# Last pair's early columns in two wide sets, both groups in one product, and a new order for the last norm, scans and scatters of the attention

## The chip, the cores and the metric

The kernel runs on one core of a Trainium2 chip. The metric is the device time of one execution in microseconds; the time before is the median of three runs. Lower is better.

## The reference, cut to what matters

An input `x` of 128 graphs with 64 nodes and 256 features goes through four layers, each with a residual and a layer norm. All arithmetic is in float32.

```python
x = layernorm(x + L0(x, adj))   # graph attention
x = layernorm(x + L1(x, adj))   # attention over 512 edges, 4 heads
x = layernorm(x + L2(x, adj))   # aggregation with A_hat, 256->512->256 with batch norms
x = layernorm(x + L3(x, adj))   # two graph convolutions, then windows of an LSTM

# L1: one score per edge and head, a softmax over the edges with one source, a weighted sum of values
e = einsum(leaky_relu(Xq[:, src] + Xq[:, dst]), a) + log(A0[src, dst] + eps)
attn = exp(e - max_by_src) / sum_by_src
Y = segment_sum(attn * Xv[:, dst], src) @ W_out.T

# L2, first step
agg = einsum('nm,bmd->bnd', A_hat, x)

# L3, after the convolutions gave h [128, 64, 256]
for p in (1, 2, 3, 4):                     # length of a window
    nw = 64 // p
    wins = h[:, :nw * p].reshape(128 * nw, p, 256)
    last = lstm_last(Wih[p-1], Whh[p-1], ..., wins)   # p steps, gates i, f, g, o
    h[:, w * p + p - 1] = last             # the last column of every window is replaced
```

For the change two places matter: the end of the edge attention (L1) with the aggregation of L2 after it, and the first step of the windows of lengths 2, 3 and 4 in the last LSTM pair. The windows of length `p` read the columns that the windows of length `p-1` have just replaced.

## The kernel before, in words

**Attention and the middle layers.** The 8192 rows are cut into 16 blocks `q` of 512 rows (`NQ`). A first long loop runs the attention of L0 and the edge scores of L1 block by block. Two blocks share one softmax `S` (`BPS = 2`), so there are eight of them. Its three parts are `l1_softmax` (lines 362 to 376: one product `L365`, an addition, two scans and a subtraction on VectorE, an exponential on ScalarE), `l1_sums` (two scans, `L380`, `L381`) and `l1_weights` (from line 383: eight transposes on TensorE, `L389`, a reciprocal `L395`, four multiplications `L397`, four indirect DMAs `L401` that scatter the weights into the table in DRAM, and two loads `ld` of that table, `L407`). For each block three further functions use the result: `v_a` (a copy of `ld` on GpSimd, `L414`, and 64 products `L422`), `v_b` (16 products with `wout`, `L436`, the residual, the layer norm with its statistics on VectorE and its powers and scaling on GpSimd, `L86` and `L100`, and a store) and `v_c` (64 small products `L456` with `aht`: the aggregation of L2).

In the loop these lag by three blocks (`LAG`). After it, what is left is the softmax of `S = 7` and `v_b(12)`, `v_c(12)` and `v_a`, `v_b`, `v_c` of blocks 13 to 15. They are traced one after another, each followed by an entry of `fill`: seven `up_block`s, products of L2's first matrix for a block whose aggregation is done (16 product instructions `L751` each), and then four larger jobs `up_job`. The last pool of the loop is closed after the softmax, and its five PSUM banks then serve the `pz` tiles of `fill`.

**Order.** `given` puts what a function traces behind the latest instruction of earlier `given` calls, on each engine by itself. An entry of `fill` isn't under `given`: the framework places its instructions where it expects an engine to be free, so parts of it can come ahead of a `given` function that was traced before it. On one engine the order is then fixed; an instruction that isn't ready holds up what is behind it.

**LSTM.** The 128 graphs are handled in eight groups of 16 (`GB`), two groups at a time: four pairs (`NP`). `H` holds a pair as `[128 features, 2 groups, 2 feature halves, 64 columns, 16 graphs]`. Windows of length 1 come first (`L1365`), then length 2 in two runs of 16 windows, length 3 with 21 windows, and length 4 with 16. The first step of a window has no hidden state: `plain` makes the three gates `g`, `i`, `o` by direct products (`begin`, `L1488`), with two halves `m` of a gate, two feature halves `k` of the input, and two groups `g`. Later steps use a seven-product scheme (`L1533`). In the trace each product of 32-bit numbers is two instructions.

A gate half of both groups fits into one PSUM bank of 512 columns when `2 * nw * GB <= 512`, that is for lengths 2 and 4. Then `joint` is true; both groups share one bank and one activation (`L1503`), but `begin` still issues one product for each group.

The last step of a window writes its result into `H` in four pieces (`L1438`): feature half 0 of group 0, half 1 of group 1, half 0 of group 1, half 1 of group 0. The next length's `plain` needs them. In the last pair there is no work of a next pair to put between, so `late_columns` splits the windows into columns that the running step doesn't write (`free`) and the others (`rest`). For gate `g` and half of gate `i` the free columns are issued ahead; the other gates go through all sets in one go. For length 3 the sets are windows 0 to 9, windows 10, 12, ... 20, and the late windows 11, 13, ... 19. For length 4 they are 0, 3, ... 15, then 1, 4, ... 13, and the late 2, 5, ... 14.

Of the kernel before, what the change touches and what calls it, by code (L numbers as in the profile page):

```python
# [21 lines left out]
KD = D // P  # L22
# [4 lines left out]
NQ = 16  # L27
# [14 lines left out]
def kernel(ctx: ExitStack, tc: tile.TileContext, i, out):  # L42
    nc = tc.nc
# [66 lines left out]
    def given(do, *args, **more):  # L110
        traced = nc.cur_bb.bb.instructions
        first = len(traced)
        with ExitStack() as order:
            for e in latest.values():
                order.enter_context(tc.issue_after(e))
            r = do(*args, **more)
        for t in traced[first:]:
            if t.engine in (mybir.EngineType.PE, mybir.EngineType.DVE, mybir.EngineType.Activation,
                            mybir.EngineType.Pool):
                latest[t.engine] = t  # L120
        return r
# [8 lines left out]
    with ExitStack() as two:  # L130
# [29 lines left out]
        class su:  # L160

            free = (NQ - NA) * 2 * QT
# [498 lines left out]
        LAG = BPS + 1  # L661
# [20 lines left out]
        for q in range(NQ):  # L682
            S = q // BPS - 1 if q % BPS == 0 else -1
# [16 lines left out]
        sums(q)  # L700
        S = NQ // BPS - 1
        given(l1_softmax, S)
        given(l1_sums, S)
        given(l1_weights, S)
        ph.close()


# [193 lines left out]
        def tile_sums(b):  # L901

            t2, t3, t4 = rooms[next(rooms_at) % len(rooms)]
            t1 = b(0, 1)
            given(nc.gpsimd.tensor_tensor, t3, b(1, 1), t1, OP.subtract)
            given(nc.vector.tensor_sub, t1, t1, b(0, 0))
            given(nc.gpsimd.tensor_tensor, t2, b(1, 1), t1, OP.subtract)
            given(nc.gpsimd.tensor_tensor, t4, b(1, 0), t2, OP.subtract)
            return [t1, t2, t3, t4]
# [12 lines left out]
        def inputs(q):  # L922
            return lambda k, n: Aq(q + n)[:, k * QT:(k + 1) * QT]
# [10 lines left out]
        def one(q):  # L934
            return lambda: up_block(q)

        def pair(q, g):
            return lambda: up_job(q, g, T[q])

        fill = [one(n) for n in range(7)] + [pair(n, g) for n in (7, 9) for g in range(2)]  # L940
        sums_at = {5: 7, 7: 9}
        for n, (do, q) in enumerate([(v_b, NQ - LAG - 1), (v_c, NQ - LAG - 1)] + [
                (do, q) for q in range(NQ - LAG, NQ) for do in (v_a, v_b, v_c)]):
            given(do, q, *[False] * (do == v_c))
            fill[n]()
            if n in sums_at:
                T[sums_at[n]] = tile_sums(inputs(sums_at[n]))
        q = NQ - LAST - 1
# [212 lines left out]
    def lbank(shape):  # L1161
        return ps.tile([P] + shape, F32, name="l", bufs=6)
# [180 lines left out]
    def gate_of(n):  # L1343
        return "ifgo".index(n), AF.Tanh if n == "g" else AF.Sigmoid

    def lstm(pair):
# [36 lines left out]
        for p in range(2, SKIP + 1):  # L1383
            w = weights_of[pair, p]
            runs = [(r, N // p // 2) for r in (0, N // p // 2)] if p == 2 else [(0, N // p)]
            nw = runs[0][1]
# [6 lines left out]
            def inp(r, s, m):  # L1393

                w0 = runs[r][0] * p
                return H[:, :, m, w0:w0 + nw * p, :].rearrange("p n (w s) b -> p n w s b", s=p)[:, :, :, s, :]
# [65 lines left out]
            begun = {}  # L1462

            def late_columns(r):

                if pair < NP - 1 or p == 2 or r:
                    return [slice(0, nw)], []
                mine, q = range(nw), p - 1
                wrote = [w for w in mine if w * p % q == q - 1 and w * p < N // q * q and (q > 2 or w * p >= N // 2)]
                step = wrote[1] - wrote[0]  # L1470
                assert wrote == list(range(wrote[0], nw, step))[:len(wrote)]
                head = wrote[0] // step * step
                free = [slice(0, head)] * (head > 0) + [slice(head + n, nw, step) for n in range(step)
                                                        if head + n != wrote[0]]
                return free, [slice(wrote[0], nw, step)]

            def begin(n, r, ms, parts):

                at, _ = gate_of(n)
                joint = 2 * nw * GB <= QT  # L1480
                for m in ms:
                    if (n, m) not in begun:
                        begun[n, m] = lbank([2, nw, GB]) if joint else [lbank([nw, GB]) for g in range(2)]
                    for g in range(2):
                        for c in parts:
                            for k in range(KD):
                                b = begun[n, m][:, g] if joint else begun[n, m][g]
                                nc.tensor.matmul(b[:, c], w.raw[0][:, k, at, m, :],  # L1488
                                                 inp(r, 0, k)[:, g, c], start=k == 0, stop=k == KD - 1)

            def plain(n, r, tiles):

                t = tiles[n] = rows()
                free, rest = late_columns(r)
                for m in (1, 0):
                    f, b = bias_of(n, m)
                    begin(n, r, (m,), rest if (n, m) in begun else free + rest)
                    banks = begun.pop((n, m))
                    if isinstance(banks, list):
                        for g in range(2):  # L1500
                            nc.scalar.activation(t[m][:, g], banks[g], f, bias=b)
                    else:
                        nc.scalar.activation(t[m], banks, f, bias=b)  # L1503
                for m in (1, 0):
                    finish(n, r, 0, tiles, m)
                    tanh(n, tiles, m)
# [69 lines left out]
            for r in range(len(runs)):  # L1576
                if p > 2:
                    yield "gap", unit
                for s in range(p):
                    last = s == p - 1  # L1580
                    if s == 0:
                        tiles = {}
                        free, rest = late_columns(r)
                        if rest:
                            given(begin, "g", r, (1, 0), free)
                            given(begin, "i", r, (1,), free)
# [139 lines left out]
    for k in range(NP):  # L1726
# [5 lines left out]
        for n in range(2):  # L1732
            g = k * 2 + n
# [61 lines left out]
```

## Time and profile before

| | us |
|---|---|
| median of three runs (lowest, highest) | 2063.9 (2063.64, 2063.99) |
| the profiled execution, whole | 2062.37 |
| its span, first to last instruction | 2060.1 |
| TensorE busy in it | 1966.5 (95%) |
| VectorE, ScalarE, GpSimd busy | 1186.3, 968.4, 807.0 |
| mean granted TensorE clock | 0.983 |

The page of the profile gives busy times and the chain of waits that ended last, followed back from the last instruction. TensorE holds 75% of that chain and VectorE 14%. Queries of the trace then show single stretches: the chain in order of time, one engine's instructions in order of time, and groups of instructions by line with their tile shapes kept apart. Times in them are microseconds from the start of the span. In the group rows the durations of matmuls overlap, since a matmul's record starts before the one ahead of it has left the array; the spacing of a run of matmuls is read from the chain, which counts no time twice.

### The profile page before, as it was taken

Reading aid. Unit: us, or ns where it says so; the run is one execution under the profiler, and the core shown is the slowest. Engines: PE = TensorE matmul, PEld = TensorE weight load, DVE = VectorE, ACT = ScalarE, POOL = GpSimd, SP = SyncE. Lnnn points to the kernel's source line nnn. Section 1 sums busy time; section 2 is a strip of 40 time slices with the busy share of each in tenths; the row PEclk is TensorE's granted clock in tenths of the full one; section 3 lists DMA queues with packets and bytes.
Section 4 is the critical chain, followed back from the end, with each engine's and each line's share of the span. In section 5 each row is a group of like instructions: output and inputs, shape, how many; then the busy total and the mean of one; then the engine's idle time right before and its main releaser. Section 6 shows DMA issues by size and latency. Waiting matters only on the chain.

```text
span 2060.1 us, 31841 instructions
## 1 busy us (share of the span) xinstructions
PE 1966.5 (95%) x11775; PEld 1387.8 (67%) x11775; DVE 1186.3 (58%) x2683; ACT 968.4 (47%) x1852; POOL 807.0 (39%) x961
## 2 busy tenths in 40 slices
PE   5999999998899999999999999999999999999996
PEld 4667677675454445687688587678587678588785
DVE  7466666554457555564566664566674466443556
ACT  3766766665245633543333644333644343533333
POOL 1123343343245534363445253245243345133254
PEclk9999999999899998999999999999999999999998
DMA  6354343332202027251232622032521032301022
GB/s 159 56 71 72 71 74 54 55 55 44 34 22 60 34 97 264 92 179 52 93 133 69 205 90 87 11 138 63 194 78 77 1 128 63 128 1 77 1 66 67
DMA packets 235962, 170.71 MB, mean 83 GB/s; under 512 B 150560, under 2 KB 213536, under 8 KB 232480
## 3 DMA queue, kind: packets, MB, share of 16 engines
q1 hardware_dynamic: 233952, 166.72, 28.8%
q8 instruction: 93, 1.52, 0.3%
q0 software_dynamic: 1024, 1.05, 0.2%
q10 hardware_dynamic: 832, 0.92, 0.1%
q14 instruction: 61, 0.50, 0.1%
HBM read 107.82 MB, written 60.82 MB: 82 GB/s over the span
## 4 chain that ended last, share of the span: by engine, by line
PE 75%; DVE 14%; POOL 4%; ACT 3%; issue 3%; DMA 1%; SPq 0%; DVEq 0%; POOLq 0%; ACTq 0%
PE l L1533 27%; PE l L1488 9%; PE l L1365 8%; PE pz L822 4%; PE e L346 3%; PE m L318 3%; PE pz L751 2%; PE g L1328 2%; PE m L321 2%; PE pz L1014 2%; PE z L355 2%; DVE ln_st L95 1%; PE g L1316 1%; PE m L253 1%; PE g L1246 1%
## 5 line engine op out<-in xcount | busy, mean ns | idle before, releaser
L1533 PE MATMUL l<-xs,wx 128*128 128x256 f32 (+1 forms) x896 | 276.7, 399 | 5.8 <-DVE gate L1552 4.8
L1533 PE MATMUL l<-hs,wh 128*128 128x256 f32 (+1 forms) x896 | 275.3, 399 | 2.7 <-DVE hs L1402 2.6
L86 POOL TENSOR_TENSOR ln_rs<-ln_rs,mhalf 128x2 f32<-128x2 f32 (+2 forms) x98 | 83.7, 854 | 456.1 <-DVE ln_rs L98 447.0
L1548 ACT ACTIVATE kept<-l 128x256 f32<-128x256 f32 (+1 forms) x224 | 88.7, 403 | 339.7 <-PE l L1533 338.5
L1533 PE MATMUL l<-H,wx 128*128 128x256 f32 (+1 forms) x672 | 210.3, 401 | 3.4 <-DVE gate L1561 3.4
L1533 PE MATMUL l<-hid,wh 128*128 128x256 f32 (+1 forms) x672 | 208.7, 399 | 0.0
L1533 PEld LDWEIGHTS l<-xs,wx 128*128 128x128 f32 x896 | 168.8, 190 | 50.1 <-POOL st L100 6.6
L1533 PEld LDWEIGHTS l<-hs,wh 128*128 128x128 f32 x896 | 169.3, 190 | 45.4 <-DVE hs L1402 5.2
L1488 PE MATMUL l<-H,wx 128*128 128x256 f32 (+4 forms) x960 | 193.6, 360 | 0.9 <-DVE H L1438 0.9
L1566 ACT ACTIVATE gate<-gate,bias 128x512 f32<-128x512 f32 (+1 forms) x280 | 170.5, 657 | 37.4 <-DVE gate L1557 31.1
L1488 PEld LDWEIGHTS l<-H,wx 128*128 128x128 f32 x960 | 160.3, 190 | 33.5 <-issue 4.1
L1365 PE MATMUL l<-H,wih 128*128 128x512 f32 x384 | 167.2, 596 | 0.0
L357 ACT ACTIVATE u<-z 128x1024 f32<-128x1024 f32 x128 | 130.4, 1025 | 63.4 <-PE z L355 62.4
L1533 PEld LDWEIGHTS l<-H,wx 128*128 128x128 f32 x672 | 125.8, 190 | 38.2 <-DVE gate L1561 7.4
L1533 PEld LDWEIGHTS l<-hid,wh 128*128 128x128 f32 x672 | 127.2, 190 | 32.0 <-issue 2.6
L1365 PEld LDWEIGHTS l<-H,wih 128*128 128x128 f32 x384 | 73.2, 191 | 89.9 <-issue 82.9
L1556 POOL TENSOR_TENSOR gate<-gate,kept 128x256 f32<-128x256 f32 (+1 forms) x84 | 65.0, 774 | 158.8 <-DVE kept L1554 158.7
L329 DVE TENSOR_TENSOR qs<-m,qs 64x256 fp32r<-64x256 f32 x128 | 54.0, 422 | 108.6 <-ACT qs L328 106.4
L1406 POOL TENSOR_TENSOR hs<-hid 128x256 f32<-128x256 f32 (+1 forms) x28 | 25.9, 926 | 200.4 <-DVE hid L1435 116.7
L355 PE MATMUL z<-gath_r,qs 128*128 128x512 f32 x256 | 100.8, 481 | 0.5 <-issue 0.4
L1460 ACT ACTIVATE gate<-cell 128x512 f32<-128x512 f32 (+1 forms) x88 | 58.6, 666 | 84.2 <-DVE cell L1452 60.5
L1550 DVE TENSOR_TENSOR gate<-l,kept 128x256 f32<-128x256 f32 (+1 forms) x112 | 49.1, 438 | 72.2 <-ACT gate L1566 44.1
(336 smaller groups left out, 3821.2 us busy)
## 6 DMA issues: line engine op xcount, KB each, us to landing
wx<-sums SPq DMA_DIRECT2D x9, 2048.0 KB
wh<-sums SPq DMA_DIRECT2D x9, 1792.0 KB
way<-st SPq DMA_DIRECT2D x54, 256.0 KB
st<-way SPq DMA_DIRECT2D x216, 64.0 KB
xin<-in_x SPq DMA_DIRECT2D x16, 512.0 KB
ld<-table SPq DMA_DIRECT2D x16, 512.0 KB
x_dram<-y SPq DMA_DIRECT2D x16, 512.0 KB
x2r<-x_dram SPq DMA_DIRECT2D x32, 256.0 KB
```

The costliest lines, as they stand in the source:

```text
L86: nc.gpsimd.tensor_tensor(dst, dst, mhalf[:, :n], OP.pow)
L318: nc.tensor.matmul(pq, xT[:, k, c * P:(c + 1) * P], wq[:, k, :], start=k == 0, stop=k == KD - 1)
L346: nc.tensor.matmul(pes[S][n * CG:(n + 1) * CG, :], apad[:, k, CG - HEADS - r0:2 * CG - HEADS - r0], u[:, k, :], start=r0 == 0 and k == 0, ...
L355: nc.tensor.matmul(z[:, k, :], L1[q]["qs"][c][:, s, k * P:(k + 1) * P], gath_r, start=True, stop=True)
L357: nc.scalar.activation(u, z, AF.Relu)
L822: nc.tensor.matmul(self.bank[at], lhs, rhs, start=first and n == 0, stop=n == len(self.terms) - 1, skip_group_check=True)
L1365: nc.tensor.matmul(b, wih1[:, k, mw * P:(mw + 1) * P], Hw[:, k], start=k == 0, stop=k == KD - 1)
L1488: nc.tensor.matmul(b[:, c], w.raw[0][:, k, at, m, :], inp(r, 0, k)[:, g, c], start=k == 0, stop=k == KD - 1)
L1533: nc.tensor.matmul(self.banks[j], lhs, rhs, start=src == 0, stop=src == 1)
L1548: nc.scalar.activation(self.keep(j), b, AF.Copy)
L1556: e.tensor_tensor(t[0][:, 1], t[0][:, 1], k[5], OP.add)
L1566: given(lambda: nc.scalar.activation(dst, dst, f, bias=b))
```

## The change

Three edits.

1. `l1_sums` and `l1_weights` of the last softmax leave their place at the end of the loop. The new order is `l1_softmax(7)`, `v_b(12)`, `up_block(0)`, `l1_sums(7)`, `up_block(1)`, `v_c(12)`, `l1_weights(7)`, and then blocks 13 to 15 as before, each function followed by the same entry of `fill` as before.
2. `late_columns` makes two contiguous sets instead of strided ones when the first late window isn't among the first few. For length 3 they are windows 0 to 10 (free) and 11 to 20 (rest). For length 4 the sets stay as they are.
3. In `begin`, when a bank is joint, one product covers both groups. This applies to lengths 2 and 4 in all four pairs.

```diff
         sums(q)
         S = NQ // BPS - 1
         given(l1_softmax, S)
-        given(l1_sums, S)
-        given(l1_weights, S)
         ph.close()
...
         fill = [one(n) for n in range(7)] + [pair(n, g) for n in (7, 9) for g in range(2)]
-        sums_at = {5: 7, 7: 9}
-        for n, (do, q) in enumerate([(v_b, NQ - LAG - 1), (v_c, NQ - LAG - 1)] + [
-                (do, q) for q in range(NQ - LAG, NQ) for do in (v_a, v_b, v_c)]):
+        given(v_b, NQ - LAG - 1)
+        fill.pop(0)()
+        given(l1_sums, S)
+        fill.pop(0)()
+        given(v_c, NQ - LAG - 1, False)
+        given(l1_weights, S)
+        sums_at = {3: 7, 5: 9}
+        for n, (do, q) in enumerate([(do, q) for q in range(NQ - LAG, NQ) for do in (v_a, v_b, v_c)]):
             given(do, q, *[False] * (do == v_c))
             fill[n]()
             if n in sums_at:
...
                 wrote = [w for w in mine if w * p % q == q - 1 and w * p < N // q * q and (q > 2 or w * p >= N // 2)]
                 step = wrote[1] - wrote[0]
                 assert wrote == list(range(wrote[0], nw, step))[:len(wrote)]
-                head = wrote[0] // step * step
-                free = [slice(0, head)] * (head > 0) + [slice(head + n, nw, step) for n in range(step)
-                                                        if head + n != wrote[0]]
-                return free, [slice(wrote[0], nw, step)]
+                if wrote[0] < step:
+                    return [slice(n, nw, step) for n in range(step) if n != wrote[0]], [slice(wrote[0], nw, step)]
+                return [slice(0, wrote[0])], [slice(wrote[0], nw)]
...
-                    for g in range(2):
+                    for g in range(1 if joint else 2):
                         for c in parts:
                             for k in range(KD):
-                                b = begun[n, m][:, g] if joint else begun[n, m][g]
-                                nc.tensor.matmul(b[:, c], w.raw[0][:, k, at, m, :],
-                                                 inp(r, 0, k)[:, g, c], start=k == 0, stop=k == KD - 1)
+                                x = inp(r, 0, k)
+                                b, x = (begun[n, m][:, :, c], x[:, :, c]) if joint else (begun[n, m][g][:, c], x[:, g, c])
+                                nc.tensor.matmul(b, w.raw[0][:, k, at, m, :], x, start=k == 0, stop=k == KD - 1)
```

## The prediction

> **What bounds the kernel now.** I read the page first: the busy line and the chain of waits that ended last.
>
> ```profile
> PE 1966.5 (95%) x11775; PEld 1387.8 (67%) x11775; DVE 1186.3 (58%) x2683; ACT 968.4 (47%) x1852; POOL 807.0 (39%) x961
> PE 75%; DVE 14%; POOL 4%; ACT 3%; issue 3%; DMA 1%; SPq 0%; DVEq 0%; POOLq 0%; ACTq 0%
> ```
>
> TensorE is the bound nearly everywhere, so an edit pays where it shortens TensorE's own stream or removes one of its gaps. The chain in order of time shows the stages that edits 2 and 3 touch (start, length, what).
>
> ```profile
> 1796.80 10.36 PE l L1488 x48
> 1831.34 10.36 PE l L1488 x48
> 1865.87 17.20 PE l L1488 x144
> 1883.07 26.05 PE l L1533 x92
> 1947.82 16.04 PE l L1488 x144
> 1963.86 13.01 PE l L1533 x60
> ```
>
> The first two are a first step of length 2 (256 columns an instruction), the third is length 3 of the last pair, the fifth length 4 of the last pair. All are unbroken TensorE with TensorE on both sides. 10.36 / 48 is 216 ns for 256 columns, 0.843 ns a column. A third of the columns of length 4 would take far less than 16.04 / 144 = 111 ns. The group rows with shapes kept apart say how narrow they are.
>
> ```profile
> L1488 PE MATMUL l<-H,wx 128*128 128x80 f32 x144 | 18.9, 273 | 0.0
> L1488 PE MATMUL l<-H,wx 128*128 128x96 f32 x96 | 14.4, 273 | 0.0
> L1488 PE MATMUL l<-H,wx 128*128 128x160 f32 x48 | 8.9, 307 | 0.0
> ```
>
> 80 and 96 columns should stream in 67 and 81 ns but are 111 ns apart: a floor per instruction. With 160 columns at 135 ns, length 3 should take 48 x 135 + 96 x 111 = 17.1 us; the chain has 17.20.
>
> For edit 1 I read TensorE in order of time, then GpSimd (start, duration, instruction; idle before it and what ended that).
>
> ```profile
> 527.69 1.07 PE L389 MATMUL m<-ident,e 128*128 128x128 f32 x4 [2.01 <-ACT e L375]
> 535.47 6.17 PE L751 MATMUL pz<-A,w 128*128 128x512 f32 x14
> 545.74 2.31 PE L456 MATMUL m<-aht,y 64*64 64x64 f32 x64 [4.10 <-POOL y L100]
> 547.98 4.65 PE L751 MATMUL pz<-A,w 128*128 128x512 f32 x6
> ...
> 533.72 1.08 POOL L401 DMA_INDIRECT table<-at,place  x1 [8.56 <-DVE at L397]
> 537.24 0.96 POOL L401 DMA_INDIRECT table<-at,place  x1 [2.43 <-DVE ln_mv L96]
> 540.12 0.96 POOL L401 DMA_INDIRECT table<-at,place  x1 [1.93 <-DMA table<-at,place]
> 542.99 0.96 POOL L401 DMA_INDIRECT table<-at,place  x1 [1.91 <-DMA table<-at,place]
> 543.98 1.05 POOL L86 TENSOR_TENSOR ln_rs<-ln_rs,mhalf 128x4 f32<-128x4 f32 x1
> 547.25 1.93 POOL L414 COPY am<-ld 128x1024 f32<-128x1024 f32 x1
> ```
>
> TensorE waits 2.01 us for the softmax and 4.10 us for the norm of block 12, which stands on GpSimd behind four scatters that take from 533.72 to 543.95.
>
> **What the Trainium skill says.** *TensorE: Matmul & The Clock Gate*, section "LDWEIGHTS (loading the stationary operand)": a weight load costs its columns / 1.2 in ns, so 107 ns for 128; the 111 ns floor agrees. The same page, "Part 1: The HAM clock gate": an idle window of about 3.4 us halves TensorE's clock until it has been busy as long again. The trace agrees: after the 4.10 us gap the 64 products take 2.31 us, against 1.09 at 571.11. *PSUM — Partial Sum Buffer*, "The four PSUM rules": one product writes at most one bank, 512 float32 columns. The joint product of lengths 2 and 4 is 2 x 16 x 16 = 512 and fits. *DMA: Bandwidth & Descriptors*, "Anatomy of one DMA — SWDGE (gpsimd) path": about 2.0 us fixed for each; the scatters land 2.13 us after issue and each waits for the one before, 2.9 us apart.
>
> **Edit 2, length 3 of the last pair.** 144 instructions become 96: 48 of 176 columns and 48 of 160, both over the floor. 48 x 0.148 + 48 x 0.135 = 13.6 us, against 17.20: 3.6 us gone. The early part shrinks from 24 x 135 + 24 x 111 = 5.9 us to 24 x 0.148 = 3.56 us, and it covers the four writes of `H`. These run in VectorE's list as one row, 1867.93 with 1.42 us, so to 1869.35; the early part would end at 1869.43. No wait is left (bound 0 to 0.3).
>
> **Edit 3, length 4 of the last pair.** 144 instructions become 72: 24 of 192 columns (162 ns) and 48 of 160 (135 ns), 10.4 us against 16.04: 5.7 us gone. The early part becomes 12 x 162 + 12 x 135 = 3.56 us, to 1951.38, and the last write of `H` ends at 1951.76 (1950.00 with 1.76). One pair of products needs only the earlier writes; 0.2 us stays (bound 0 to 0.5). Both stages are followed by TensorE's own work. ScalarE has 6.4 us and VectorE 6.4 us of work in those 16, so neither becomes the bound. The DMA round trip of an output group that VectorE waits for after 1977 begins behind instructions that TensorE feeds and moves with them. Sum for the last pair: 3.6 + 5.7 - 0.2 = 9.1 us on the path.
>
> **Edit 3 elsewhere.** From 256 to 512 columns nothing is won: 96 products of 512 columns of length 1 take 41.20 us, 429 ns each, twice 216. Fewer weight loads cost nothing as they lie beside the stream. But a joint product waits for both groups. At the start of length 4 in pairs 0 to 2, TensorE issues four instructions at 1031.86, before the last write of `H`, and goes on at 1033.18. The first joint product needs the third write of four, which ends near 1032.7; from there 10.36 us run through, to 1043.1, where 1033.18 + 44 x 0.216 gave 1042.7. So +0.4 us, three times: 1.2 us (bound 0 to 1.8). At length 2 the columns read first were written earlier, and the second run's too: nothing.
>
> **Edit 1.** From 522.28 to 552.64, where `v_a(13)` starts, TensorE's work at full clock is 16 x 0.216 + 32 x 0.429 + 8 x 0.214 + 1.09 = 20.0 us; 10.4 us are lost, 6.1 in the two gaps and 4.3 to the halved clock. Afterwards: `v_b(12)`'s products are ready at once and go first (to 525.7), then two `up_block`s of 6.87 us (to 539.5). VectorE does the softmax, to 527.0, then the norm (4.3 us) among block statistics, then the two scans. GpSimd has nothing ahead of the norm, which is done by about 537; so `v_c(12)` and the transposes follow without a gap, to 542.2. Then the reciprocal and products (2 us), four scatters (544.3 to about 554.5) and, behind them on GpSimd, the copy `L414` for `v_a(13)` (1.93): ready at about 556. That is the new wait: what stood behind the scatters was the norm, now it is this copy. SP gains nothing and loses nothing: block 12's store comes earlier, the two loads of `ld` later, and `v_a(14)` that reads them came 26.7 us after `v_a(13)`.
>
> Between 542.2 and 556 TensorE can do `up_block(2)` and `(3)`, 13.7 us, if they are placed ahead of `v_a(13)`. Before, the framework put ten instructions of `up_block(1)` ahead of `v_c(12)`, 10.3 us of work behind the transposes where 14.4 were needed: it expected the scatters about 4 us too early. With the same error `v_a(13)` comes 4 us too early: a gap of 4 us and 2 to 3 us of halved clock, 6.9 in all instead of 10.4. I take 3.5 us gained. Bounds: -2.5 us if only `up_block(2)` comes ahead (gap near 9), +10 if no gap is left.
>
> **Sum.** The span goes from 2060.1 by -9.1 + 1.2 - 3.5 = -11.4 to 2048.7; with the 2.3 us around it (2062.37 - 2060.1) 2051.0. The median of the runs is 1.5 us over the profiled execution, so 2052.5.
>
> **Rivals.**
> - *The copy for `v_a(13)` takes the place of the norm in full.* For it: one queue on GpSimd, and the scatters start 10 us later than before. Against: two more blocks can cover it. Edit 1 then costs 2.5: 2063.9 - 9.1 + 1.2 + 2.5 = 2058.5.
> - *The scatters vanish behind the blocks.* Against: the misplaced `v_c(12)` above. 2063.9 - 9.1 + 1.2 - 10 = 2046.0.
> - *Length 4 gives its gain back* to the output's DMA round trip that VectorE waits for up to 1984.89. Against: its transfer starts from VectorE instructions that move along. 2052.5 + 5.5 = 2058.0.
> - *Slower: the joint product is held by writes it doesn't read.* Its operand spans both groups, with the columns just being written in between. If it waited for those, run 2 of length 2 would start after the four `H` writes, 1835.06 where TensorE is ready at 1831.34 (3.7 us), and run 1 about 1 us late; four pairs make 18.8 us, 2071.3. It decides from 11.4 us, 2.9 a pair. Against: at 1865.87 the strided set of windows 10, 12, ... is read between columns that are written until 1869.35, and TensorE doesn't stop.
>
> **How the numbers follow.** The forecast has 0.55 (own range 2049 to 2056), the rivals in their order 0.18, 0.12, 0.08, 0.07. With all bounds against it the gain is 8.5 - 1.8 - 2.5 = 4.2, 2059.7; with all for it 9.3 + 10 = 19.3, 2044.6. I take 2046 to 2060. A measurement here can't tell less than about 0.2%, 4.1 us, from no change. The first and third rival stand close to that line, so faster 0.83, the same 0.11, slower 0.06.
>
> **What would show it.** In the changed trace: 96 and 72 instructions in the last pair's two first steps, taking 13.6 to 13.9 and 10.4 to 10.9 us; no gap ahead of `v_c(12)`; a gap of about 4 us ahead of `v_a(13)`'s products, ended by GpSimd's copy; the first joint product of length 4 at about 1032.7 in the old count. Wrong would be a gap at a start of length 2, or last steps that end less than 8 us sooner, measured from the start of length 3 of the last pair.

## The result and the profile after

The changed kernel takes 2052.35 us (median of four runs, 2049.48 to 2053.71); the kernel before took 2063.94 beside it (four runs, 2063.64 to 2065.31). The ratio is 0.9941, with a 95% interval of 0.9923 to 0.9958. The profiled execution has a span of 2050.9 us against 2060.1, at the same mean TensorE clock, 0.983.

The page of the changed kernel, busy times and then the shares of the chain that ended last:

```profile
PE 1959.1 (96%) x11391; PEld 1329.2 (65%) x11391; DVE 1185.8 (58%) x2683; ACT 968.4 (47%) x1852; POOL 809.7 (39%) x961
PE 74%; DVE 13%; POOL 4%; ACT 4%; issue 3%; DMA 2%; SPq 1%; POOLq 0%; ACTq 0%; DVEq 0%
```

TensorE issues 384 instructions fewer, the other engines the same number. Its busy time falls by only 7.4 us. For 264 of those that went, two products of 256 columns became one of 512, which takes as long as the two.

The chain in order of time, at the stages shown before (start, length, what):

```profile
1797.74 10.30 PE l L1491 x24
1832.21 10.30 PE l L1491 x24
1866.69 13.68 PE l L1491 x96
1880.37 26.00 PE l L1535 x92
1945.07 10.83 PE l L1491 x72
1955.90 12.96 PE l L1535 x60
```

Length 2 has half the instructions and the same time, 10.30 us against 10.36, and nothing waits at its two starts. Length 3 of the last pair goes from 17.20 to 13.68 us and length 4 from 16.04 to 10.83. From the start of the one to the end of the other it is 89.21 us, against 97.99.

At length 4 of the first pair the chain runs through the writes of `H`, as it did before, and leaves them after the third instead of the fourth:

```profile
1030.76 0.42 DVE H L1441
1031.18 0.60 DVE hT L1321
1031.78 0.84 DVE H L1441 x2
1032.62 0.04 issue
1032.67 7.13 PE l L1491 x16
```

The first joint product starts at 1032.67, 0.05 us after the third write of `H` ended.

The end of the edge attention, TensorE and then GpSimd in order of time (start, duration, instruction; in brackets the idle time before it and what ended that):

```profile
543.08 1.16 PE L456 MATMUL m<-aht,y 64*64 64x64 f32 x64
544.17 0.66 PE L389 MATMUL m<-ident,e 128*128 128x128 f32 x4
...
545.96 12.18 PE L749 MATMUL pz<-A,w 128*128 128x512 f32 x28
560.65 1.16 PE L422 MATMUL m<-am,v 64*64 64x64 f32 x64 [2.50 <-POOL am L414]
...
573.10 2.08 PE L456 MATMUL m<-aht,y 64*64 64x64 f32 x64 [0.80 <-POOL y L100]
```

```profile
533.96 1.03 POOL L86 TENSOR_TENSOR ln_rs<-ln_rs,mhalf 128x4 f32<-128x4 f32 x1 [5.07 <-DVE ln_rs L98]
535.10 3.45 POOL L100 TENSOR_SCALAR y<-y,ln_rs 128x256 f32<-128x256 f32 x4
548.94 1.09 POOL L401 DMA_INDIRECT table<-at,place  x1 [10.39 <-DVE at L397]
...
557.70 0.96 POOL L401 DMA_INDIRECT table<-at,place  x1 [1.92 <-DVE st L755]
558.67 1.93 POOL L414 COPY am<-ld 128x1024 f32<-128x1024 f32 x1
...
572.50 2.17 POOL L100 TENSOR_SCALAR y<-y,ln_rs 128x256 f32<-128x256 f32 x4
```

Both old gaps are gone: `v_c(12)` and the transposes follow their predecessors. The norm of block 12 is done at 538.55, ten microseconds ahead of the first scatter. The queue of GpSimd now holds up the copy of `v_a(13)`, and TensorE waits 2.50 us for it. A second, shorter wait of 0.80 us stands ahead of `v_c(13)`; the 64 products after it take 2.08 us instead of 1.16.

In some spells the record grants TensorE only half of its clock (0.50); its products then take about twice as long (from 561.74 four of 512 columns take 3.45 us; at full clock, from 578.98, sixteen take 7.13). Two stretches of the changed kernel (window, its length, busy time and in brackets the instructions of TensorE, of its weight loads, VectorE, ScalarE and GpSimd; then the granted clock, DMA share, GB/s):

```profile
562.20:565.40 3.20, 3.20 (x5) 1.35 (x4) 0.69 (x1) 1.49 (x3) 0.00 (x0) 0.50 1.28 152
573.10:575.20 2.10, 1.86 (x65) 1.38 (x65) 0.00 (x0) 0.00 (x0) 2.10 (x4) 1.00 0.02 4
```

After the wait of 2.50 us the clock is at half. At `v_c(13)` it is full: its products take 2.08 us because they come in four groups, each when GpSimd has finished one of the four pieces of `y` (`L100`, 0.54 us apart).

Put together, the span moved by -9.2 us as follows. The changed stages gave -3.5 (length 3), -5.2 (length 4), +1.2 (joint products in pairs 0 to 2) and -5.0 (end of the attention), together -12.5. Code that both kernels share took 3.3 back: the last score products ended 3.7 us later (524.91 against 521.19), the code from L2's output to the last pair lost 1.0, and the rest of the last pair gained 1.4. The experiments show that 1.5 to 1.8 of the 5.0 us is such a difference too, and not the edit's.

### The profile page after: what moved, and what is told of

It reads as the page before. It is cut to its first block, busy times and chain, and to the rows that moved or that the text cites. A ratio compares the mean times of both kernels' runs of the same rounds, so it can differ in the third digit from the quotient of the medians.

```text
span 2050.9 us, 31078 instructions
## 1 busy us (share of the span) xinstructions
PE 1959.1 (96%) x11391; PEld 1329.2 (65%) x11391; DVE 1185.8 (58%) x2683; ACT 968.4 (47%) x1852; POOL 809.7 (39%) x961
## 4 chain that ended last, share of the span: by engine, by line
PE 74%; DVE 13%; POOL 4%; ACT 4%; issue 3%; DMA 2%; SPq 1%; POOLq 0%; ACTq 0%; DVEq 0%
PE l L1535 27%; PE l L1491 9%; PE l L1368 8%; PE pz L820 4%; PE e L346 3%; PE pz L749 3%; PE m L318 3%; PE g L1331 2%; PE pz L1017 2%; PE m L321 2%; PE z L355 2%; PE m L253 2%; PE m L436 1%; PE g L1319 1%; DVE ln_st L95 1%
## 5 line engine op out<-in xcount | busy, mean ns | idle before, releaser
L1568 ACT ACTIVATE gate<-gate,bias 128x512 f32<-128x512 f32 (+1 forms) x280 | 170.6, 657 | 37.4 <-DVE gate L1559 31.1
L1491 PE MATMUL l<-H,wx 128*128 128x512 f32 (+4 forms) x576 | 183.7, 475 | 2.2 <-DVE H L1441 2.2
L1535 PEld LDWEIGHTS l<-H,wx 128*128 128x128 f32 x672 | 125.9, 190 | 42.8 <-issue 7.4
L1491 PEld LDWEIGHTS l<-H,wx 128*128 128x128 f32 x576 | 100.9, 190 | 76.2 <-issue 53.6
```

Source lines behind the costliest of these rows:

```text
L1491: nc.tensor.matmul(b, w.raw[0][:, k, at, m, :], x, start=k == 0, stop=k == KD - 1)
L1535: nc.tensor.matmul(self.banks[j], lhs, rhs, start=src == 0, stop=src == 1)
L1568: given(lambda: nc.scalar.activation(dst, dst, f, bias=b))
```

## The experiments

In what follows, "the stretch" is measured in the trace, from the end of the last 16 score products to the first of the 60 products of L2's output (`L1014` before, `L1017` after). Before it is 144.58 us and after 139.59. Where an expectation counts from the start of those score products (143 for after, 148.1 for before), it is 1.9 to 3.6 us more, as their own clock differs; the readings here leave that out. Gains in us that stand beside a ratio are worked out from the ratio.

**Each edit alone.** Each of the three kernels is the kernel before with one edit of the diff: only edit 1, only `late_columns`, only `begin`.

> Edit 1 alone; the last pair as before. My theory: the stretch from the last score products (the final row of 16 e products, 517.66 before) to the first of the 60 products of line 1014 takes 143 us instead of 148.1, with a gap of 2 to 4 us ahead of the products of v_a(13); the last pair's first steps stay at 17.2 and 16.0 us; ratio to before about 0.9980. Rival (the gain of edit 1 is only a run-to-run difference): the stretch stays within 1 us of 148.1, ratio 1.0000.

Measured: 2056.74 us (20 runs) against 2061.26 for the kernel before (31 runs), a ratio of 0.9977 (0.9971 to 0.9984): 4.7 us, with bounds of 3.3 and 6.0. The stretch is 139.61 us, 5.0 less. That is far from a stretch that stays within 1 us, so the rival is out. Its wait is the one of the changed kernel:

```profile
557.89 1.16 PE L422 MATMUL m<-am,v 64*64 64x64 f32 x64 [2.52 <-POOL am L414]
```

> Edit 2 alone. My theory: the first step of length 3 in the last pair takes 13.6 to 13.8 us instead of 17.20, from 96 instructions instead of 144; length 4 stays at 16.0; all that follows comes 3.5 us earlier; ratio about 0.9983. Rival (VectorE's chain at the end of length 3 gives it back): the stage shrinks but the start of length 4 comes less than 2 us earlier.

Measured: 2055.55 us (10 runs), 0.9976 (0.9966 to 0.9985), which is 4.9 us (3.1 to 7.0). The chain shows length 3 shortened and length 4 as it was:

```profile
1864.59 13.68 PE l L1487 x96
...
1942.98 16.04 PE l L1487 x144
```

From the start of the one to the start of the other it is 78.39 us, against 81.95 before, so VectorE gives nothing back and the rival is out.

> Edit 3 alone. My theory: length 4 of the last pair 10.4 to 10.9 us instead of 16.04; in pairs 0 to 2 the time from the 80 products before the start of length 4 to the seven-product run after it grows from 44.24 to 44.6 us; net about 4.1 us gained, ratio 0.9980. Rival (a joint product is free everywhere): the stretch in pairs 0 to 2 stays at 44.2 us and the net gain is 5.2 us.

Measured: 2054.08 us (6 runs), 0.9966 (0.9953 to 0.9978), which is 7.0 us (4.5 to 9.7). Here length 3 is as it was and length 4 is short:

```profile
1864.35 17.20 PE l L1489 x144
...
1946.29 10.83 PE l L1489 x72
```

In pairs 0 to 2 the time from the 80 products to the seven-product run is 44.61, 44.62 and 44.48 us, against 44.24 before: the joint product isn't free there.

Edits 2 and 3 do in their stages what they do together, 3.5 and 5.2 us (4.1 with the three waits of 0.4). The timed gains are larger than that, and the three add up to 16.6 us where the whole change gives 11.6. The trace shows where the surplus lies: from the end of the score products to the first step of length 2 the code of the second and third kernel is that of before, yet this part takes 337.70 and 337.90 us in them and 341.06 before. Two of the places (before, then edit 3 alone):

```profile
777.34 5.17 PE L1316 MATMUL g<-hT,wg 128*128 128x512 f32 x8
...
808.84 6.51 PE L1365 MATMUL l<-H,wih 128*128 128x512 f32 x12
```

```profile
777.51 4.18 PE L1316 MATMUL g<-hT,wg 128*128 128x512 f32 x8
...
807.82 5.42 PE L1365 MATMUL l<-H,wih 128*128 128x512 f32 x12
```

The products are the same; the half-clock spells last longer in the first kernel. The stretches show it, in the columns explained above (before, then edit 3 alone):

```profile
770.00:820.00 50.00, 46.46 (x496) 28.90 (x497) 31.19 (x76) 19.65 (x33) 25.74 (x32) 0.86 0.69 248
```

```profile
770.00:820.00 50.00, 45.54 (x501) 27.83 (x502) 32.16 (x77) 20.09 (x33) 25.94 (x32) 0.95 0.71 253
```

The stretch at the end of the attention isn't free of this either: with its code unchanged it takes 142.82 us with edit 2 alone and 143.04 with edit 3 alone, where the kernel before has 144.58. With edit 1 alone the part from the score products to length 2 takes 337.30 us, and with all three 337.35. So in this part edits 2 and 3 gain over 3 us without touching its code, and edit 1 on top of them only some 0.5.

**The joint product only where the columns are split**, so not in pairs 0 to 2:

```diff
+                wide = joint and bool(late_columns(r)[1])
...
-                    for g in range(1 if joint else 2):
+                    for g in range(1 if wide else 2):
```

> The changed kernel, but with one product for both groups only where the windows are split into sets (length 4 of the last pair); elsewhere one product per group, as before. My theory: the stretch in pairs 0 to 2 goes back from 44.6 to 44.24 us, length 4 of the last pair stays at 10.8; 1.1 us faster than the changed kernel, ratio to before about 0.9936. Rival (the wait of the joint product lies beside other work): the same time as the changed kernel, and the sums of the stage differ by less than 0.2 us in each pair.

Measured: 2048.64 us (four runs), 0.9941 (0.9924 to 0.9957). From the start of the 80 products ahead of it to the first seven-product run, length 4 takes 44.24 us in pairs 0 to 2 of the kernel before, 44.62 to 44.64 after, and 44.24 here. Length 4 of the last pair keeps its 10.82 us. So the joint product costs 0.37 to 0.40 us in each of those pairs, 1.16 in all, and this kernel has them back; the timed runs can't tell it from the changed kernel (0.9941 both). The kernels below build on this one, except where stated.

**The scatters further back**, behind `v_a(13)`, and then behind `v_b(13)` as well:

```diff
         given(v_c, NQ - LAG - 1, False)
+        given(v_a, NQ - LAG)
+        fill.pop(0)()
         given(l1_weights, S)
```

The second kernel has `given(v_b, NQ - LAG)` and one more `fill.pop(0)()` after these two lines.

> The kernel with joint products only where the windows are split, and the weights of the last softmax (transposes, scatters, loads) moved one function further back, behind v_a(13). My theory: the copy for v_a(13) no longer stands behind the scatters, so its 2.5 us gap goes; the norm of block 13 now does, and as the framework expects the scatters about 4 us too early a gap of 1 to 4 us comes ahead of v_c(13). The stretch from the end of the last score products to the 60 products of line 1014 takes 138 to 140 us (139.5 in the changed kernel). Rival (the gap comes from the scatters' own transfer holding the table, not from GpSimd's order): the gap ahead of v_a(13) stays.

Measured: 2051.58 us against 2064.74, 0.9940 (0.9923 to 0.9956): no better than 0.9941. The wait of `v_a(13)` is gone, which rules the rival out, and a longer one stands ahead of `v_c(13)`, whose norm is now behind the scatters:

```profile
565.68 2.32 PE L456 MATMUL m<-aht,y 64*64 64x64 f32 x64 [3.17 <-POOL y L100]
```

The stretch is 141.08 us, 1.5 more than with the order of the change, and longer than expected. The next part, up to length 2, takes 2.8 us less than with the order of the change (194.98 and 197.81), with code that is the same in both; that makes the result even.

> As the run before, but the weights two functions further back, behind v_b(13). My theory: neither the copy for v_a(13) nor the norm of block 13 waits for the scatters; the next that does is the copy for v_a(14), which also needs the loads of the table. If the blocks of products cover it, no gap above 1 us is left and the stretch takes 136.5 to 138 us. Rival (the loads come too late): a gap of 3 to 8 us ahead of v_a(14) and a stretch over 140 us.

Measured: 2058.15 us (8 runs), 0.9972 (0.9961 to 0.9983). The stretch is 148.07 us: the rival is right here. The chain shows what it is:

```profile
573.82 2.14 DMA table<-at,place
575.95 0.02 issue
575.97 0.52 SPq L407
576.49 0.05 issue
576.54 9.52 DMA ld<-table
...
586.21 1.94 POOL am L414
```

The loads `ld` of the scattered table take 9.52 us, and now `v_a(14)`, which reads them, comes too soon. Ahead of later products TensorE waits 2.14, 2.21 and 2.78 us. With the scatters this late the price is 8.5 us in the stretch.

**Without the last scatters** (the changed kernel, with `range(EC if S < NQ // BPS - 1 else 0)` in their loop):

> The changed kernel without the four scatters of the last softmax: the weights of blocks 14 and 15 stay those of an older softmax. My theory: GpSimd reaches the copy for v_a(13) about 10 us sooner, the gap of 2.5 us ahead of its products goes, and so does a part of the 0.8 us ahead of v_c(13); the stretch takes 136 to 137.5 us instead of 139.5. Rival (the gap is an effect of the order on TensorE alone): it stays within 1 us.

Measured: 2044.34 us (one run); the stretch is 134.76 us, below the range expected, and there is no wait ahead of `v_a(13)` or `v_c(13)`. The four scatters still cost the changed kernel 4.8 us in the stretch. The records account for them: TensorE is busy for 133.65 of 139.59 us there and for 132.39 of 134.76 here, so it is idle 3.6 us longer (its two waits of 2.50 and 0.80, and the pauses between the four groups of `v_c(13)`) and busy 1.3 us longer, which goes with the half clock after the first wait.

**More products ahead of `v_a(13)`**: `up_block(2)` and `(3)` are traced ahead of it, and in the second kernel `(4)` too; two or three later places go without.

```diff
         given(l1_weights, S)
-        sums_at = {3: 7, 5: 9}
+        fill.pop(0)()
+        fill.pop(0)()
+        fill.insert(6, lambda: None)
+        fill.append(lambda: None)
+        sums_at = {1: 7, 3: 9}
```

> The changed kernel with joint products only where the windows are split, and two blocks of products (2 and 3) traced ahead of v_a(13) instead of one behind it; v_a(15) and v_c(15) have none behind them. My theory: TensorE has 32 product instructions between the transposes and v_a(13) instead of 28, so the gap of 2.5 us there shrinks to about 0.8; the stretch takes 137.5 to 139 us (139.5). Rival (what is used up early is missing later): a new gap of over 1.5 us ahead of v_c(15) or v_b(15) and a stretch of 139.5 us or more.

Measured: 2043.29 us (four runs, 2040.72 to 2047.94) against 2061.68 (seven runs): 0.9905 (0.9888 to 0.9921). The wait is shorter, not as short as expected, and later in the stretch TensorE waits for VectorE for 3.5 us in sum, where the changed kernel waits for 2.3:

```profile
556.33 1.16 PE L422 MATMUL m<-am,v 64*64 64x64 f32 x64 [1.65 <-POOL am L414]
...
622.14 1.13 PE L820 MATMUL pz<-w,w 128*128 128x512 f32 x2 [1.24 <-DVE wq L845]
...
635.22 1.48 PE L820 MATMUL pz<-lb,SW 128*128 128x512 f32 x2 [2.24 <-DVE kept L832]
```

> As the run before with three blocks ahead of v_a(13). My theory: 48 instructions cover the scatters and the copy in full, no gap ahead of v_a(13); v_a(13) itself comes 4 us later, which costs nothing by itself; the stretch takes 136.5 to 138.5 us. Rival (later gaps): the attention functions of blocks 14 and 15 run short of covering products, gaps of 3 us or more in sum after 590 and a stretch of 139.5 us or more.

Measured: 2045.78 us (four runs), 0.9919 (0.9903 to 0.9936). No wait ahead of `v_a(13)` is left:

```profile
543.10 19.91 PE L749 MATMUL pz<-A,w 128*128 128x512 f32 x46
562.93 1.16 PE L422 MATMUL m<-am,v 64*64 64x64 f32 x64
```

Its later waits make 3.8 us in sum, as its rival said, but not a stretch of 139.5. The stretch is 138.64 and 136.47 us in the two, within or just below what was expected. Both kernels beat the one before. They are to be compared with the kernel that they build on (0.9941, 0.9924 to 0.9957; stretch 139.53): the first is clear of it, the interval of the second overlaps with it. The intervals of the two overlap as well, so which is better stays open. The stretch explains only 0.9 of the 7.4 us that the first gains on that kernel by the ratios, and 3.1 of the 4.5 us of the second. The profiled execution of the first was the slowest of its four (2047.94 us), so its trace shows only a part of its gain; where the rest comes from isn't shown.

**The floor per instruction.** Length 4 of the last pair, in the kernel before, with every set cut in two (288 instructions of 48 or 32 columns), and then with the late set alone cut (192 of 96, 80, 48 and 32):

```diff
+                if p == SKIP:
+                    n, step = wrote[0], 2 * step
+                    free = [slice(x, nw, step) for x in range(step) if x not in (n, n + step // 2)]
+                    return free, [slice(n, nw, step), slice(n + step // 2, nw, step)]
```

> The kernel before, with every set of length 4 in the last pair cut into two: 288 instructions of 48 or 32 columns in place of 144 of 96 or 80, the same columns in all. My theory (a floor of 111 ns an instruction, the weight load): the step takes 288 x 0.111 = 32 us instead of 16.04, and the whole 16 us more. Rival (strided columns cost 1.3 ns each whatever their number): 16 us, the same time.

Measured: 2107.53 us (one run). The chain, and then stretches of the stage, in the columns explained above:

```profile
1950.41 58.18 PE l L1492 x288
```

```profile
1950.50:1953.50 3.00, 3.00 (x29) 3.00 (x29) 2.96 (x8) 1.72 (x4) 0.00 (x0) 1.00 0.01 3
...
1965.00:1975.00 10.00, 10.00 (x49) 10.00 (x48) 0.00 (x0) 1.19 (x2) 0.00 (x0) 0.50 0.00 0
```

A cost by columns would have kept the stage at 16 us, so that rival falls. But it isn't 32 us either: after some 3 us at full clock the granted clock is 0.50 to the end of the stage, though TensorE has no idle moment in the records. A stretch counts each instruction that reaches into it, two or three too many here; by their starting times the instructions are 111 ns apart at full clock and 213 ns at half, so the 204 ns of the next expectation is a little small.

> The kernel before, with only the late set of length 4 in the last pair cut into two: 192 instructions of 96, 80, 48 and 32 columns in place of 144 of 96 and 80. My theory (a floor of 111 ns an instruction as long as the clock is full): 192 x 0.111 = 21.4 us instead of 16.04 if the granted clock stays at 1.0; if the monitor halves it here too, as it did with 32 and 48 columns alone (204 ns an instruction), more, with the clock at 0.5 in the windows. Rival (the cost is by column, 1.3 ns each): 16 us.

Measured: 2074.73 us (one run); the stage takes 31.03 us, not 21.4. The first 48 instructions are those of 96 and 80 columns, the next 48 those of 48 and 32, and the last 96 mix all four. The stretches follow that order; the line ahead of them is one of the kernel before, with 96 and 80 columns throughout:

```profile
1948.00:1956.00 8.00, 8.00 (x74) 8.00 (x73) 3.73 (x9) 3.14 (x7) 3.68 (x6) 1.00 0.01 3
```

```profile
1945.50:1950.50 5.00, 5.00 (x47) 5.00 (x47) 3.77 (x9) 1.68 (x4) 1.53 (x2) 1.00 0.01 2
1950.60:1955.60 5.00, 5.00 (x47) 5.00 (x47) 0.00 (x0) 1.38 (x2) 2.06 (x4) 1.00 0.02 3
1956.00:1976.00 20.00, 20.00 (x96) 20.00 (x96) 2.70 (x4) 3.32 (x5) 0.00 (x0) 0.50 0.08 26
```

At full clock the same number of instructions fits into 5 us whether they have 96 and 80 columns or 48 and 32, so the floor, 111 ns from start to start, holds for both. Then the clock falls, and the spacing is 213 ns: 96 x 0.111 + 96 x 0.213 = 31.1 us.

What the floor is made of was not tested by itself, since all these products have weights of 128 columns. A fixed cost of that size for every instruction is out: the 64 products of `v_a`, of 64 columns each, take 1.09 us together, 17 ns each. That it is the weight load rests on the 107 ns that the prediction cites.

## Why the prediction was right, step by step

**Length 3 of the last pair: right.** 13.68 us against 13.6 worked out from 0.843 ns a column, with no wait for `H`. The kernel with this edit alone shows the same 13.68.

**Length 4 of the last pair: right, with one term small.** The stream of 10.4 us was right. The wait for the last write of `H` was priced at 0.2 us with a bound of 0.5; the stage shows 10.83, so about 0.4. By their starting times the first pair of late products begins at 1948.64 and the next at 1949.06, each 0.05 us after a write of `H`, the third (to 1948.59) and the fourth (to 1949.01). So the pair that needs only earlier writes did go ahead of the last one, but it had to wait for the third, and the first four late instructions lose 0.41 us in sum against an even spacing of 136 ns. From start of length 3 to the end of length 4's first step the gain is 8.78 us, where 9.1 was predicted.

**Joint products elsewhere: right.** The first one starts at 1032.67 where "near 1032.7" was said, and the three pairs lose 0.39, 0.37 and 0.40 us where 0.4 each was said. The kernel without joint products there shows that they are the cause. At length 2 there is no cost and no gain.

**Edit 1: the mechanism right, its sizes off both ways.** The wait moved to the copy `L414` for `v_a(13)`, as predicted, but is 2.50 us and not 4: the framework placed 30 product instructions between the first transposes and it (2 and 28 in the lines above), where an error as large as the earlier one would have left about 22 of the 32. The short wait of 0.80 us ahead of `v_c(13)`, and the 0.9 us that its four groups take longer, were not in the working. The stretch gains 5.0 us against the kernel before, and 3.2 to 3.5 against the two kernels with edit 2 or 3 alone, whose stretch has the same code (142.82 and 143.04 to 139.6); 3.5 was predicted. That this fits so well is partly luck, as a wait that came out too large and one that was left out offset each other. The timed run of this edit alone gives 4.7. Over the longer part up to length 2 the traces leave 0.4 to 3.7 us, depending on which of the two clock patterns of unchanged code it is set against.

One reading of the working doesn't carry what is put on it. It takes the 2.31 us of `v_c(12)` as the sign of the halved clock. The granted clock was 0.50 there, but these products too come in four groups as GpSimd finishes its pieces, and `v_c(13)` takes 2.08 us in that way at full clock. The six products after `v_c(12)` are the better sign: 4.65 us, where six at 429 ns take 2.6.

**The rivals.** The slower one, a joint product held by writes that it doesn't read, is out: both runs of length 2 in the last pair start without a gap. That length 4 gives its gain back to the output's round trip is out too: from the seven-product run after it to the end it is 95.0 us, against 96.24. That the copy takes the norm's place in full, or that the scatters vanish, is excluded by the 2.50 us of the new wait: the first asked for a gap near 9, the second for none.

**The sum.** 11.4 us were predicted, 11.6 are the difference of the medians. This agreement is closer than the working deserves: in the traces the changed stages gave 12.5 us and code that is the same in both took 3.3 back. What decides whether the part from the end of the score products to the first step of length 2 takes 337 or 341 us isn't settled. One kernel varies as much by itself: the 31 runs of the kernel before that stand beside the single edits go from 2058.02 to 2063.76 us, with a mean granted clock of 0.988 in the fastest and 0.984 in the slowest. Single gains here are therefore known to about 2 to 3 us from timed runs, however narrow their intervals. In the traces the first steps of lengths 3 and 4 repeat within 0.1 us, the stretch at the end of the attention only within 2.

## What to carry to other kernels

Products whose columns stream in less time than one weight load cost a floor each, here 111 ns at full clock and 213 at half: make them wider by larger sets or by joining groups, but only where the joined operand doesn't add a wait for its last part, as it did by 0.4 us in each of three pairs. Work that is moved behind an in-order queue doesn't lose its cost; ask what stands behind it next, and give the engine that waits enough other products by writing them ahead, rather than leaving it to the placement. The stage in the trace is a better measure of a few microseconds than the whole time when half-clock spells elsewhere move by as much; but look at the granted clock within the stage first, and compare traces that have the same.

## What was not expected of the hardware

Narrow products lower the granted clock without any idle time. With 48 and 32 columns behind weight loads of 128 columns the clock was full for some 3 us in one kernel and some 5 us in the other, then 0.50 to the end of the stage, 213 ns an instruction; in the second kernel it stayed there although the last 96 instructions have all four widths. With 80 and 96 columns alone (the kernel before, the line of 74 instructions in 8 us) it stayed at 1.00. The Trainium skill, *TensorE: Matmul & The Clock Gate*, "Part 1: The HAM clock gate", ties the gate to how busy the array has been and shows it at idle time. Here the records show TensorE and its weight loads busy throughout, so by this measurement an unbroken row of instructions isn't enough. What in such a row lowers the clock was not tested.

The same page says that the window of the gate runs freely, so that the number of slow products varies from run to run. That agrees with the 3.3 us between two executions of the same code above (341.06 and 337.7) and their clocks of 0.86 and 0.95 in the same 50 us, though whether a window that runs freely is the cause is open.

A wait of 2.50 us was followed by a spell at half clock (0.50 from 562.20 to 565.40 in the changed kernel), where the prediction counted with an idle window of about 3.4 us.

The two loads of the scattered table took 9.52 us to land when something waited for them; in the order of the change TensorE has other work meanwhile, and no wait stands ahead of `v_a(14)`.
